# A third product of sums of vertical attention done as an addition on VectorE, with new due steps

## The chip, the cores and the metric

The kernel runs on one core of a Trainium2 chip. The core has five engines with a queue each: TensorE (PE, matrix products; PEld are its weight loads), VectorE (DVE), ScalarE (ACT), GpSimd (POOL) and SyncE (SP), which here only issues DMA transfers. An engine runs its instructions in the order in which they were written; semaphores hold an instruction back until what it needs is there. The metric is the device time of one execution in microseconds (us), lower is better.

## What is computed

Eight images of 64 x 64 pixels with 256 channels go through two layers; all is in fp32. The first layer, cut to what matters:

```python
q, k = split(x @ w_qkv + b_qkv)          # 2 x 256 channels; v = k
ctx_h = sdpa(h_windows(q), h_windows(k), h_windows(v))   # channels 0..127, windows of 8 rows
ctx_v = sdpa(v_windows(q), v_windows(k), v_windows(v))   # channels 128..255, windows of 8 columns
bias  = depthwise_conv3x3(hard_swish(v)) + dw_bias
x1    = hard_swish(concat(ctx_h, ctx_v) + bias) @ w_out + b_out
# sdpa(q,k,v): softmax(q k^T / sqrt(32)) v, four heads of 32, windows of 512 pixels
```

The second layer is global attention over the 4096 pixels of an image with 32 channels: f, g and h are products of x1 with weights divided by their spectral norm; the output is gamma * (softmax(g f^T) h @ wv + bv) + x1.

## The kernel before

Pixels are cut into eight blocks of 512. A **unit** is a window of one attention: eight horizontal ones (h, one for a block of rows), eight vertical ones (v) and two global ones (l, 2048 queries each) per image. A unit goes through steps, four in an h or v unit and 32 in an l unit. In a step TensorE makes scores of 128 keys against 512 queries for four heads at once (tile `s`, line 679, or 860 in an l unit); ScalarE takes two exponentials of 128x1024 (line 477, `weights_of`) and leaves the weights `p`, four heads side by side, in a ring of three buffers (pool `ptp`). One step later TensorE multiplies the weights of the step before with the values into `num` (line 696, or 876). Everything else is filled in between: a "fill".

The softmax's denominators are the sums of the weights over all keys. TensorE makes them as products with a matrix of ones (`sums`, line 714), 32 output rows for each head, in two halves of 256 columns. For an h or v unit it doesn't sum all four chunks so: VectorE first adds chunks 0 and 1 (`add`, line 705, 128x2048) into `acc`, which has one buffer, and three terms are left: chunk 2, chunk 3 and `acc`. For an l unit VectorE adds all 32 chunks (lines 885 and 887), and one term is left (line 896). ScalarE copies the sums out of PSUM (`copy_sums`, line 497); VectorE transposes, takes reciprocals, spreads them and multiplies (`norm`, lines 487 to 490 and 731).

Around it: projections of x to q and k (`project`, line 262, evicted by ScalarE on lines 551 to 570); the values' transpose on VectorE (line 632), written to DRAM and fetched by SP (lines 637 and 648); clip and swish into the padded image `hv` (lines 597 and 604), rings of two buffers for the lower channels and three for the upper, with borders set by POOL (lines 589 to 595, 609 and 610); the convolution, one tap on ScalarE (line 618) and eight taps on VectorE (line 622) for each pair of blocks and each half of the channels; a v unit's shuffle through DRAM (lines 737 and 742); join, clip and context (lines 755, 759 and 764); the projections to f, g and h (lines 783 and 810), of which h is transposed (line 824) and copied (line 825); and the output (lines 915, 262 and 925). Projections, sums and transposes share one PSUM bank, so that a fill waits for the eviction of the fill before.

The instructions' order is found at build time by a planner, `Flow`. Each piece of work is a task with a due step, tasks that it `needs` (their modelled end counts) and tasks that it comes `after` (only order counts). In each step the planner issues the scores, then the held values, and fills the engines' queues with waiting tasks by due step and by costs written at the head of the file. The dictionary `DUE` holds the due steps; most are relative to a unit's first step. Images overlap: projections and clips of the next image are made during the global attention of the one before, and so is its unit h[0], which stands ahead of the l units. A second copy of the whole attention (`exact`), with maxima taken out before the exponentials, stands behind a branch and isn't run with these inputs.

Whether an h or v unit adds chunk 2 on VectorE as well is already a switch, `adds_h` and `adds_v`: with it `acc` takes chunk 2 in a second addition (due at step `add2` of the unit) and two terms are left.

Of the kernel before, what the change touches and what calls it, by code (L numbers as in the profile page):

```python
# [23 lines left out]
NB = N // TB  # L24
# [7 lines left out]
def quad(r):  # L32
# [4 lines left out]
QH = 4  # L37

DUE = dict(
    near_k=-4, near_q=-3, near_values=-13, clip=-2, swish=4,  # L40
    conv_h0=13, conv_h1=10, conv_h2=7, conv_h3=16, conv_v0=-3, conv_v1=-3, conv_v2=14, conv_v3=9,
    tap=-5, join_h=14, join_hl=10, join_v=12, context=0, norm=2, release=0, sums=-2, add=1, adds_h=0, adds_v=0, add2=1, apart=4,
    fg0=-7, fg2=11, fg3=20, h0=3, h1=14, values_v=-3, near0=3, spread0=12, spread1=61,
    conv_first=-10, far_swish=1,
)
INSIDE = 4
AHEAD = 16
# [1 line left out]
HV = (2, 3)  # L49
# [216 lines left out]
def tile_attention_blocks(  # L266
# [108 lines left out]
    sums = prep.tile([P, NF + C + 1], F32, name="sums")  # L375
# [31 lines left out]
    def attention(images, load_x, out_rows, exact):  # L407
# [533 lines left out]
        flow = Flow()  # L941
# [103 lines left out]
        def behind(tag, bufs, first, *last):  # L1045
# [2 lines left out]
                first.after += queue[-bufs]  # L1048
            queue.append(last)

        loads = []

        def load(im, i, *tasks):
# [8 lines left out]
        def product_pieces(f, n, *end):  # L1062
            pieces = [(partial(f, k), [("pe", PROD / HALVES)]) for k in range(n * HALVES)]
            pieces[-1] = (pieces[-1][0], [("pe", PROD / HALVES), *end])
            return pieces

        def inside_due(i, far):

            n = i + min(i, INSIDE) + far
            return DUE["spread0"] + (DUE["spread1"] - DUE["spread0"]) * n // (NB + INSIDE)  # L1070

        for n, im in enumerate(ims):
            last = ims[n - 1] if n else None
            h, v, l = im.h, im.v, im.l
            near, far, sw, cv, pv = {}, {}, {}, {}, {}
            im.near, im.far = near, far
            for i in range(NB):
                u = h[i]
                after = [near[i - 1, 0], near[i - 1, 2]] if i else []
                after += [sw[i - QH, 0], pv[0, i - QH]] if i >= QH else []  # L1080

                inside = last and 0 < i <= INSIDE
                start = last.l[0].t if last else 0
                ready = start if inside else last.v[0].t + DUE["near0"] if last else max(0, u.t - 4)
                if i >= QH:
                    ready = max(ready, h[i - QH].t + 4)
                due = start + inside_due(i, 0) if inside else None
                for m in (0, 2):
                    near[i, m] = flow.add(
                        "pe", product_pieces(partial(im.project, i, m), 2, ("act", EVICT)),  # L1090
                        (u.t + DUE["near_k" if m else "near_q"]) if due is None else due, [], after, ready, True,
                    )
                early = start + inside_due(i, 0) if i in (1, 2) else u.t
                turned_v = flow.add(
                    "dve", [(partial(im.values, 0, i), [("dve", TAP), ("sp", ISSUE), ("dma", VIA)])],
                    min(early + 8, u.t + DUE["near_values"]), [near[i, 2]], [], min(early, u.t - 8),
                )
                pv[0, i] = flow.add(
                    "sp", [(partial(im.fetch_values, 0, i), [("sp", 4 * ISSUE), ("dma", FETCH)])], 0,
                    [turned_v], [], max(0, min(early, u.t - 3)),  # L1100
                )
                for m in (1, 3):
                    after = [sw[i - 1, 1]] if m == 3 and i else []
                    ready, due = (start, start + inside_due(i, 1)) if last else (0, u.t + 1)
                    end = (("act", 2 * (VIEW if m == 1 else EVICT)),)
                    far[i, m] = flow.add(
                        "pe", product_pieces(partial(im.project, i, m), 2, *end), due,
                        [], after, ready, True,
                    )
                for half in range(2):  # L1110
                    if half:
                        due = start + inside_due(i, 1) + DUE["far_swish"] if last else u.t + 6
                    else:
                        due = start + inside_due(i, 1) + DUE["swish"] - 2 if inside else u.t + DUE["swish"]
                    cl = flow.add(
                        "act", [(partial(im.clip, i, half), [("act", EVICT)])],
                        due + DUE["clip"] - 2, [far[i, 3] if half else near[i, 2]],
                        [cv[i // 2 - HV[half], half]] if i // 2 >= HV[half] else [],
                    )
                    sw[i, half] = flow.add(  # L1120
                        "dve", [(partial(im.swish, i, half), [("dve", SWISH), ("dma", HALO)])],
                        due, [cl], [sw[k, half] for k in (i - 1,) if i],
                    )
                    p = (i - 2) // 2 if i % 2 == 0 else i // 2 if i == NB - 1 else -1
                    if p >= 0:
                        k = 2 * p
                        due = (v if half else h)[k].t + DUE[f"conv_{'hv'[half]}{p}"]
                        if half and last and k == 0:
                            due = min(due, start + inside_due(2 * HV[1], 0) + DUE["conv_first"])
                        tap = flow.add(  # L1130
                            "act", [(partial(im.conv, p, half, (0,)), [("act", EXP)])],
                            due + DUE["tap"], [sw[q, half] for q in range(k, min(NB, k + 3))],
                            last.results[k] if last else [],
                        )
                        taps = [
                            (partial(im.conv, p, half, (q,)), [("dve", TAPS)]) for q in range(1, 9)
                        ]
                        cv[p, half] = flow.add("dve", taps, due, [tap])
            for i in range(NB):
                turned_v = flow.add(  # L1140
                    "dve", [(partial(im.values, 1, i), [("dve", TAP), ("sp", ISSUE), ("dma", VIA)])],
# [6 lines left out]
            context = {}  # L1148
            for kind, us in enumerate((h, v)):
                for i, u in enumerate(us):  # L1150
                    due = u.t + (DUE["join_v"] if kind else DUE["join_h"] if i < NQ else DUE["join_hl"] + 4 * (i - NQ))
# [9 lines left out]
            for kind, k in (("f", 0), ("f", 1), ("h", 0), ("f", 2), ("f", 3), ("h", 1)):  # L1161
                after = order[-1:]
                if kind == "f":
                    due = l[0].t + DUE[f"fg{max(0, k - 1) and k}"]
                    pf[k] = flow.add(
                        "pe", product_pieces(partial(im.project_fg, k), 2, ("act", EVICT)),
                        due, combined + [context[z, i] for z in range(2) for i in (2 * k, 2 * k + 1)],
                        [*after, *([turned[0]] if k == 3 else []), *([pf[0]] if k == 2 else [])], 0, True,
                    )
                    order.append(pf[k])  # L1170
                    pf[k] = flow.add("sp", [(partial(im.fetch_fg, k), [("sp", 10 * ISSUE), ("dma", FETCH)])], 0, [pf[k]])
                else:
                    due = l[0].t + DUE[f"h{k}"]
                    ph[k] = flow.add(
                        "pe", product_pieces(partial(im.project_h, k), 2, ("act", EVICT)),
                        due, [context[z, i] for z in range(2) for i in range(4 * k, 4 * k + 4)],
                        [*after, *([pf[2]] if k == 1 else [])], 0, True,
                    )
                    order.append(ph[k])
                    turned[k] = flow.add(  # L1180
                        "turn", [(partial(im.turn_h, k), [("pe", TURN), ("act", EVICT)])], due + 1, [ph[k]],
                        bank=True,
                    )
# [72 lines left out]
    xv = xT.rearrange("b (k p) n -> b p k n", p=P)  # L1256
    ov = out.rearrange("(b m p) n -> b m p n", m=2, p=P)
    attention(
        range(B),
        lambda b, i: xv[b, :, :, i * TB : (i + 1) * TB],  # L1260
# [18 lines left out]
    with tc.If(fine < 2 * P):  # L1279
        with tc.For_i(0, B) as b:  # L1280
            attention(
                [b],
                lambda b, i: xT[bass.ds(b, 1)].rearrange("o (k p) n -> p (o k) n", p=P)[
                    :, :, i * TB : (i + 1) * TB
                ],
                lambda b, m: out[bass.ds(b * C + m * P, P), :],
                exact=True,
            )
# [45 lines left out]
```

## Time and profile before

| What | us |
|---|---|
| median of three runs | 3434.96 (3431.73 to 3436.49) |
| the profiled execution's own time | 3432.03 |
| its span on the core | 3430.1 |
| PE busy | 3368.3 |
| DVE busy | 2729.4 |
| ACT busy | 2666.5 |
| POOL busy | 63.1 |

The span begins with the first and ends with the last recorded instruction of the core; the run's own time is 1.9 us more. An engine's busy time is the union of its instructions' times. The end of a matmul is modelled, so that a wait inside a run of matmuls can be counted as busy. The granted TensorE clock was 0.997 of full speed. An fp32 matmul of the program shows in the trace as two records. In the groups, a line gives the engine, the operation, the tile written and those read, shapes, the number of records, their busy time, the mean ns of one, and the engine's idle time just before them with what ended it.

### The profile page before, as it was taken

The numbers are of one execution on the slowest core, as the hardware profiler recorded it, in microseconds if no ns is written. First come the engines' busy times: TensorE is split into PE (matmuls) and PEld (weight loads), VectorE is DVE, ScalarE is ACT, GpSimd is POOL, SyncE is SP. The second block draws the span as 40 slices with busy tenths as digits, with TensorE's granted clock in tenths as the row PEclk, the third lists the DMA queues.
The fourth block names the chain that finished last, engine by engine and source line by source line (L and its number), as shares of the span: only waits on it lengthen the run. The fifth ranks groups of instructions, "written<-read, shape, count | busy, mean of one in ns | idle before, by whom it ended". The sixth has DMA issues, their size and how long they took to land.

```text
span 3430.1 us, 80125 instructions
## 1 busy us (share of the span) xinstructions
PE 3368.3 (98%) x34804; PEld 1154.6 (34%) x34804; DVE 2729.4 (80%) x2276; ACT 2666.5 (78%) x3235; POOL 63.1 (2%) x266
## 2 busy tenths in 40 slices
PE   8999999999999999999999999999999999999997
PEld 3333333333333333333333333333333333333322
DVE  4897798777897778968789687896878968788776
ACT  5788777887787877878778787787877878778875
POOL 0000000000000000000000000000000000000000
PEclk9999999999999999999999999999999999999998
DMA  2131103311123111231112311123111231122200
GB/s 71 57 99 51 56 28 88 96 46 50 44 72 100 48 45 44 72 106 41 50 50 75 98 37 47 56 81 92 40 38 59 84 86 40 38 72 65 70 31 26
DMA packets 249417, 209.94 MB, mean 61 GB/s; under 512 B 26080, under 2 KB 190432, under 8 KB 249056
## 3 DMA queue, kind: packets, MB, share of 16 engines
q1 hardware_dynamic: 246816, 204.18, 20.4%
q8 instruction: 275, 4.51, 0.6%
q10 hardware_dynamic: 2240, 0.56, 0.1%
q14 instruction: 86, 0.70, 0.1%
HBM read 99.78 MB, written 83.89 MB: 54 GB/s over the span
## 4 chain that ended last, share of the span: by engine, by line
PE 79%; DVE 14%; ACT 4%; issue 2%; DMA 1%; DVEq 0%; ACTq 0%; SPq 0%
PE s L679 16%; DVE acc_l L887 12%; PE pq L262 11%; PE s L860 10%; PE num_l L876 8%; PE num_v L696 7%; PE num_h L696 7%; PE s L262 6%; PE sum_h L714 5%; PE sum_v L714 5%; PE pf L783 2%; DVE act L622 1%; ACT p_l L477 1%; ACT p_h L477 1%; PE s L915 1%
## 5 line engine op out<-in xcount | busy, mean ns | idle before, releaser
L887 DVE TENSOR_TENSOR acc_l<-acc_l,p_l 128x2048 f32<-128x2048 f32 x480 | 1099.8, 2291 | 230.7 <-ACT p_l L477 207.6
L477 ACT ACTIVATE p_l<-s 128x1024 f32<-128x1024 f32 x1024 | 992.9, 1026 | 200.6 <-PE s L860 143.7
L622 DVE SCALAR_TENSOR_TENSOR act<-hv,dw_sb,act 128x1024 f32<-128x1024 f32 x512 | 655.7, 1281 | 22.7 <-ACT act L618 8.6
L860 PE MATMUL s<-gq,f 32*128 32x512 f32 x4096 | 625.9, 640 | 1.4 <-ACT ot_l L925 0.9
L477 ACT ACTIVATE p_h<-s 128x1024 f32<-128x1024 f32 x512 | 494.5, 1023 | 94.9 <-PE s L679 70.9
L477 ACT ACTIVATE p_v<-s 128x1024 f32<-128x1024 f32 x512 | 496.0, 1023 | 92.7 <-PE s L679 86.9
L876 PE MATMUL num_l<-p_l,h_sb 128*32 128x512 f32 x4096 | 546.4, 605 | 2.4 <-ACT nums_l L891 2.1
L262 PE MATMUL pq<-x,wqkv_sb 128*32 128x256 f32 x8192 | 524.0, 382 | 2.1 <-ACT qh L551 0.8
L262 PEld LDWEIGHTS pq<-x,wqkv_sb 128*32 128x32 f32 x8192 | 261.3, 110 | 368.9 <-issue 201.9
L679 PE MATMUL s<-qh,kh 32*128 32x512 f32 x2048 | 319.0, 641 | 10.3 <-ACT qh L551 5.9
L679 PE MATMUL s<-qv,kv 32*128 32x512 f32 x2048 | 317.7, 640 | 0.2 <-ACT p_v L477 0.2
L860 PEld LDWEIGHTS s<-gq,f 32*128 32x128 f32 x4096 | 192.9, 182 | 298.6 <-issue 284.7
L696 PE MATMUL num_v<-p_v,vs 128*32 128x512 f32 x2048 | 272.7, 605 | 2.5 <-DMA vs<-kvia 2.5
L696 PE MATMUL num_h<-p_h,vs 128*32 128x512 f32 x2048 | 271.6, 602 | 3.5 <-ACT nums_l L891 1.9
L262 PE MATMUL s<-act,wout_sb 128*32 128x512 f32 x2048 | 227.0, 595 | 0.0
L925 ACT ACTIVATE ot_l<-s,bias_o 128x512 f32<-128x512 f32 x128 | 81.2, 684 | 174.2 <-PE s L262 162.7
L876 PEld LDWEIGHTS num_l<-p_l,h_sb 128*32 128x32 f32 x4096 | 80.7, 108 | 387.5 <-issue 370.7
L705 DVE TENSOR_TENSOR acc_h<-p_h,p_h 128x2048 f32<-128x2048 f32 x64 | 146.5, 2290 | 44.1 <-ACT p_h L477 30.9
L705 DVE TENSOR_TENSOR acc_v<-p_v,p_v 128x2048 f32<-128x2048 f32 x64 | 146.6, 2291 | 36.8 <-ACT p_v L477 36.8
L679 PEld LDWEIGHTS s<-qh,kh 32*128 32x128 f32 x2048 | 97.1, 183 | 182.2 <-issue 146.7
L679 PEld LDWEIGHTS s<-qv,kv 32*128 32x128 f32 x2048 | 101.6, 182 | 162.2 <-issue 157.9
L714 PE MATMUL sum_h<-p_h,ones 128*32 128x256 f32 x2048 | 137.3, 380 | 4.2 <-ACT kv L570 4.2
(125 smaller groups left out, 2417.8 us busy)
## 6 DMA issues: line engine op xcount, KB each, us to landing
x<-in_xT SPq DMA_DIRECT2D x92, 512.0 KB, 3.9
kvia<-kt SPq DMA_DIRECT2D x128, 256.0 KB, 2.4
vs<-kvia SPq DMA_DIRECT2D x512, 64.0 KB, 2.1
out<-ot_l SPq DMA_DIRECT2D x128, 256.0 KB, 2.1
via_v<-nums_v SPq DMA_DIRECT2D x64, 256.0 KB, 2.1
shuf_v<-via_v SPq DMA_DIRECT2D x256, 64.0 KB, 2.0
f<-fg SPq DMA_DIRECT2D x256, 64.0 KB, 2.0
gq<-fg SPq DMA_DIRECT2D x64, 64.0 KB, 2.0
```

The costliest lines, as they stand in the source:

```text
L262: nc.tensor.matmul(out[quad(r), :], lhsT=lhsT[:, quad(r)], rhs=rhs, start=start, stop=stop)
L477: nc.scalar.activation(pt[:, 2 * z : 2 * z + 2, :], sc[z], AF.Exp, scale=scale)
L622: nc.vector.scalar_tensor_tensor(o, src, wt, o, ALU.mult, ALU.add)
L679: nc.tensor.matmul(row_of(sc, r), lhsT=k[quad(r), c * P : (c + 1) * P], rhs=q[quad(r), :], start=True, stop=not exact,)
L696: nc.tensor.matmul(u["num"][quad(r), :], lhsT=vs[kind, i][:, r, c, :], rhs=u[c][:, r, :], start=(c == 0), stop=(c == 3),)
L705: nc.vector.tensor_add(u["acc"], u["acc"] if c == 2 else u[0], u[c])
L714: nc.tensor.matmul(u["sum"][quad(r), cols], lhsT=ones[:, :D], rhs=pt[:, r, cols], start=(k == 0), stop=(k == len(of) - 1),)
L783: nc.tensor.matmul(pf[quad(r), cols], lhsT=wcomb[:, k, quad(r % 2)], rhs=act_of(2 * p + r // 2, k, cols), start=(k == 0), stop=(k == 1),)
L860: nc.tensor.matmul(row_of(sc, r), lhsT=f4[quad(r), c * P : (c + 1) * P], rhs=gq[quad(r), z, :], start=True, stop=not exact,)
L876: nc.tensor.matmul(u["num"][quad(r), :], lhsT=h_sb[:, c, :], rhs=u[c][:, r, :], start=(c == 0), stop=(c == 4 * NB - 1),)
L887: nc.vector.tensor_add(u["acc"], u["acc"], u[c])
L925: nc.scalar.activation(ot, po, AF.Identity, bias=bias_o[:, m : m + 1])
```

## The change

With `adds_v=1`, vertical units add chunk 2 into `acc` on VectorE, and TensorE's products with ones take two terms, chunk 3 and `acc`, in place of three. Horizontal units stay as they are. Twenty-odd due steps have other values, among them those of the convolutions of each pair of blocks, the clips and swishes, the sums, the near projections and f, g, h. Three orders are changed: a clip into an `hv` buffer now comes after the convolution that used that buffer before, over the border between images too (`convs` counts pairs over all images); `project_fg` of pair 2 comes after the fetch of pair 1 in place of pair 0; and `project_h` of each half comes after a fetch of f and g (of pair 0 for the first, of pair 2 for the second, which had it before).

```diff
 DUE = dict(
-    near_k=-4, near_q=-3, near_values=-13, clip=-2, swish=4,
-    conv_h0=13, conv_h1=10, conv_h2=7, conv_h3=16, conv_v0=-3, conv_v1=-3, conv_v2=14, conv_v3=9,
-    tap=-5, join_h=14, join_hl=10, join_v=12, context=0, norm=2, release=0, sums=-2, add=1, adds_h=0, adds_v=0, add2=1, apart=4,
-    fg0=-7, fg2=11, fg3=20, h0=3, h1=14, values_v=-3, near0=3, spread0=12, spread1=61,
-    conv_first=-10, far_swish=1,
+    near_k=-4, near_q=-1, near_values=-13, clip=-12, swish=-1,
+    conv_h0=17, conv_h1=15, conv_h2=7, conv_h3=14, conv_v0=1, conv_v1=10, conv_v2=14, conv_v3=12,
+    tap=-9, join_h=13, join_hl=10, join_v=12, context=0, norm=2, release=0, sums=0, add=1, adds_h=0, adds_v=1, add2=3, apart=4,
+    fg0=-7, fg2=5, fg3=20, h0=1, h1=10, values_v=-4, near0=-4, spread0=12, spread1=61,
+    conv_first=3, far_swish=1,
 )
...
+        convs = {}
         loads = []
...
                         due + DUE["clip"] - 2, [far[i, 3] if half else near[i, 2]],
-                        [cv[i // 2 - HV[half], half]] if i // 2 >= HV[half] else [],
+                        [k for k in (convs.get((i // 2 - HV[half] + n * NB // 2, half)),) if k],
...
-                        cv[p, half] = flow.add("dve", taps, due, [tap])
+                        cv[p, half] = convs[p + n * NB // 2, half] = flow.add("dve", taps, due, [tap])
...
-                        [*after, *([turned[0]] if k == 3 else []), *([pf[0]] if k == 2 else [])], 0, True,
+                        [*after, *([turned[0]] if k == 3 else []), *([pf[1]] if k == 2 else [])], 0, True,
...
-                        [*after, *([pf[2]] if k == 1 else [])], 0, True,
+                        [*after, pf[2 * k]], 0, True,
```

## The prediction

> **What bounds the kernel now.** I read the page's totals first, then busy time by stage, then the groups that the change touches, then the order of time inside one unit of vertical attention.
>
> ```profile
> span 3430.1 us, 80125 instructions
> ...
> PE 3368.3 (98%) x34804; PEld 1154.6 (34%) x34804; DVE 2729.4 (80%) x2276; ACT 2666.5 (78%) x3235; POOL 63.1 (2%) x266
> ```
>
> TensorE is busy all through; VectorE and ScalarE have a fifth free on average. By stage of the second image (horizontal, vertical and global attention; columns are length, then busy time of PE, PEld, DVE, ACT):
>
> ```profile
> 480.80:593.30 112.50, 111.24 (x1212) 39.80 (x1208) 98.22 (x102) 85.72 (x109) 4.06 (x20) 1.00 0.26 78
> 593.30:693.70 100.40, 99.33 (x1065) 35.72 (x1061) 77.41 (x84) 80.20 (x97) 0.18 (x2) 1.00 0.33 90
> 693.70:901.90 208.20, 207.93 (x2082) 67.96 (x2078) 164.18 (x97) 166.63 (x201) 3.35 (x10) 1.00 0.14 41
> ```
>
> VectorE is fullest in the horizontal stage (87%) and has 23.0 us idle in the vertical one. The groups of the change:
>
> ```profile
> L714 PE MATMUL sum_v<-p_v,ones 128*32 128x256 f32 x2048 | 135.2, 379 | 6.4 <-ACT h_sb L825 6.4
> L714 PE MATMUL sum_v<-acc_v,ones 128*32 128x256 f32 x1024 | 78.7, 379 | 0.0
> L705 DVE TENSOR_TENSOR acc_v<-p_v,p_v 128x2048 f32<-128x2048 f32 x64 | 146.6, 2291 | 36.8 <-ACT p_v L477 36.8
> L622 DVE SCALAR_TENSOR_TENSOR act<-hv,dw_sb,act 128x1024 f32<-128x1024 f32 x512 | 655.7, 1281 | 22.7 <-ACT act L618 8.6
> ```
>
> A row's 379 ns is no price, since matmuls overlap. The price is start to start, on TensorE's timeline of one vertical unit:
>
> ```profile
> 1057.57 1.14 PE L679 MATMUL s<-qv,kv 32*128 32x512 f32 x8
> ...
> 1059.64 1.37 PE L679 MATMUL s<-qv,kv 32*128 32x512 f32 x8
> ...
> 1061.94 1.51 PE L679 MATMUL s<-qv,kv 32*128 32x512 f32 x8
> ...
> 1064.38 1.14 PE L679 MATMUL s<-qv,kv 32*128 32x512 f32 x8
> ...
> 1066.33 1.05 PE L714 MATMUL sum_v<-p_v,ones 128*32 128x256 f32 x16
> 1067.19 0.61 PE L714 MATMUL sum_v<-acc_v,ones 128*32 128x256 f32 x8
> 1067.62 1.05 PE L714 MATMUL sum_v<-p_v,ones 128*32 128x256 f32 x16
> 1068.49 0.61 PE L714 MATMUL sum_v<-acc_v,ones 128*32 128x256 f32 x8
> 1069.03 1.14 PE L679 MATMUL s<-qv,kv 32*128 32x512 f32 x8
> ```
>
> A unit takes 11.46 us. Steps of scores and values alone last 2.07, then 2.30 and 2.44: the last two contain a wait of 0.2 to 0.4 us for ScalarE's exponentials, which "busy" hides. Eight recorded ones-matmuls cost 0.43 us. Last, two lines from the waits and from the end of the chain:
>
> ```profile
> PE sum_v L714 <- ACT h_sb L825: 6.4, 6, 1.1
> ```
>
> ```profile
> 3394.10 2.30 DVE acc_l L887
> ```
>
> The final global stage is a chain of VectorE additions, one every 2.4 us; work put in front of it shows in full.
>
> [...]
>
> **The change, part by part.**
>
> Products removed. The built order has 64 units with 16 products for sum_v instead of 24, so 16 records fewer per unit: 2 x 0.43 = 0.86 us. 64 x 0.86 = **-55.2 us**. Weights loads overlap and go with them.
>
> Additions added. 64 x 2.29 = 146.6 us of VectorE, 18.3 per image. The moved due steps make room: in the built order of a steady image the vertical stage keeps 9 of its 18 taps (-9 x 1.28 = -11.5), one normalization (-2.4) and one context product (-0.7) go past its end. VectorE there: 77.4 + 18.3 - 11.5 - 2.4 - 0.7 = 81.1. The stage's PE length: seven of its eight sums stand inside it, 7 x 0.86 = 6.0, and two projections (16 x 0.216 = 3.5) go to the horizontal stage: 100.4 - 6.0 - 3.5 = 90.9. So 89% full. The horizontal stage gets 8 taps: 98.2 + 10.2 = 108.5 in 112.5 + 3.5 = 116.0, 93% full. Hidden by TensorE's work; what little room is left is the question. The eight taps have a place: VectorE now idles 9.7 us in the second horizontal unit of that stage, and the changed order puts seven taps (9.0 us) there. Lags in this stage may cost 0 to 3 us an image (no gain: no work leaves it); I take 0.4 x 7 = **+3**.
>
> Inside a vertical unit. Sum products now stand one step later (after the next unit's second scores), so the steps are 2.07, 2.30, 2.44 and a last of 4.65 - 0.86 = 3.79: 10.60 us. ScalarE needs 8 x 0.92 + 2 x 0.59 + 0.72 = 9.3 of it. VectorE: two additions 4.6, normalization 2.5, join and context 1.4, transpose 0.7 = 9.2. The accumulator has one buffer, so the next first addition starts only when the sums are read, 0.1 us after the fill; then normalization, a join, the second addition: 0.1 + 2.3 + 2.5 + 0.7 + 2.3 = 7.9 us. The weights ring of three makes ScalarE's exponential of the next unit's second chunk wait for that addition; it wants to start at about 8.0. Behind it stand all later exponentials, and TensorE waits for those. Margin 0.1 us. Bounds: 0 to 0.5 us a unit; I take 0.1: **+6**. The sums themselves start at 8.8, after it.
>
> The wait for h_sb. Now the transposed h's eviction holds the one fill bank and the sum behind it waits 1.1 us. In the changed order a whole step lies between: **-6.4**, or 0 if another eviction takes its place.
>
> First image. Its vertical stage holds on VectorE 16 additions, 19 taps, 8 normalizations and 21 small operations (16 x 2.29 + 19 x 1.28 + 8 x 2.4 + 21 x 0.69 = 95 us) in 101.1 - 6.0 - 1.7 = 93.4 of TensorE (one projection of 1.7 leaves): over full. **+3**, between 0 and 6.
>
> Last image. The chain of additions gets two small operations more in front of it (1.4 us) and four taps in the unit before: **+2**, between 0 and 5.
>
> Guards and other due steps. ScalarE's clips and their memsets on POOL stand as many units behind the last tap of the buffer that they replace as now; near projections as far ahead of their scores; 0. On SP a normalization's store and its shuffled fetch go out some 6 us later; the fetch, behind the next transpose's store, lands some 1.5 us into the following unit, and the join reads it at 8: 6 us of cover. Without it the join would hold VectorE for what is missing. The store of values goes at most a place later and its fetch has two units.
>
> Sum: -55.2 + 3 + 6 - 6.4 + 3 + 2 = -47.6. The profiled execution took 3432.0 us (span 3430.1), so 3384.4; the median of the runs is 2.9 above it: **3387 us**.
>
> **Rivals.**
>
> A, the gain half lost: the second addition is late by 0.5 us in every vertical unit through the ring of weights, 64 x 0.5 = 32 instead of 6, giving 3413. For it: the margin of 0.1 us, and ScalarE already waited 53.3 us for acc_l through the same ring. Against it: taps are nearly gone from these units.
>
> B, slower: VectorE becomes the bound because its idle time can't be filled. Horizontal and vertical stage leave it 7.5 + 9.8 = 17.3 us per image; now it idles 14.3 + 23.0 = 37.3 there. If 30 of that were dependency gaps that stay, each of seven images would pay 12.7 for a gain of 8.8: 3435 + 27 = 3462. It decides from 26.1 us of unfillable idle time. For it: waits for clips and copies (85.7 and 84.1 us over all). Against it: five horizontal units in a row now run with gaps of 0.3 to 1.3 us in 11 to 23, so such queues do fill up.
>
> C, more than the products: the lags don't appear and the h_sb wait goes: -61.6, 3373.
>
> That the products stay is excluded by the built order.
>
> **How the numbers follow.** Forecast 0.55 (3373 to 3400 by its bounds), C 0.14, A 0.18, B with smaller losses that cancel the gain 0.13. Holding 8 in 10 takes in C and A, with some room on both sides: 3366 to 3418. Faster by over 0.2%, which is about what a measurement of this kernel can tell (below 3428): 0.88; within 0.2%: 0.03; slower: 0.09.
>
> **What would show it.** The group sum_v from p_v with 1024 records; acc_v with 128; vertical stages near 91 us with VectorE near 81; units 10.6 apart. The step on the ring is wrong if ScalarE's p_v waits long for acc_v (A: over 25 us). B shows as horizontal stages over 120 us with VectorE at 95% and TensorE waiting for p_h or sums for acc. The first vertical stage should be longer than the others, and the chain should still end in acc_l. The prediction falls if those stages are not shorter than now by 6 us or more.

## The result and the profile after

The changed kernel took 3422.61 us (median of seven runs, 3418.80 to 3425.57) against 3434.96 (3431.73 to 3437.63, seven runs): a ratio of 0.9966, interval 0.9954 to 0.9977. It is faster by 0.34%, a quarter of the 48 us that the forecast had. The profiled execution took 3424.4 us and its span is 3422.6, 7.5 less than the span before; stages are compared within these two spans. Each kernel's stages are read from one execution, and the changed kernel's seven lie up to 6.8 us apart, so a difference of a few us between the totals of two traces may be chance.

The totals on the page of the changed kernel:

```profile
span 3422.6 us, 78296 instructions
...
PE 3334.3 (97%) x33780; PEld 1126.0 (33%) x33780; DVE 2860.2 (84%) x2340; ACT 2665.0 (78%) x3235; POOL 63.5 (2%) x266
```

TensorE has 34.0 us less to do, but the span is only 7.5 shorter: 26.5 us of new idle time on TensorE, and more that "busy" hides. The groups of the change, in the changed kernel:

```profile
L705 DVE TENSOR_TENSOR acc_v<-p_v,p_v 128x2048 f32<-128x2048 f32 x64 | 146.7, 2292 | 87.1 <-issue 60.5 <-PE sum_v L714 17.3 <-ACT p_v L477 9.3
...
L705 DVE TENSOR_TENSOR acc_v<-acc_v,p_v 128x2048 f32<-128x2048 f32 x64 | 146.2, 2284 | 4.8 <-ACT p_v L477 4.8
...
L714 PE MATMUL sum_v<-p_v,ones 128*32 128x256 f32 x1024 | 80.1, 385 | 0.8 <-ACT fg L792 0.8
L714 PE MATMUL sum_v<-acc_v,ones 128*32 128x256 f32 x1024 | 79.2, 381 | 3.1 <-DVE acc_v L705 3.1
```

The 1024 records are gone and the 64 additions are there. The first line holds the surprise: before the *first* addition of a unit VectorE now idles 87.1 us in all, and before it was 36.8, all of it for the weights. Now it waits for the sums of the unit before, which read the one accumulator. The list of releasers names them for 17.3 us only, and has no releaser for 60.5 ("issue"); but each of the 42 waits that make up the 87.1 ends 0.12 to 0.14 us after the last of those sums.

The first two stages of the second image (horizontal, vertical; length, then busy time of PE, PEld, DVE, ACT):

```profile
506.20:621.80 115.60, 114.52 (x1280) 41.49 (x1276) 107.22 (x109) 88.63 (x112) 6.56 (x20) 1.00 0.26 81
621.80:713.40 91.60, 89.81 (x884) 30.24 (x880) 80.45 (x82) 77.20 (x92) 0.18 (x2) 1.00 0.32 91
```

And the first image's vertical stage, one line of the kernel before and one of the changed kernel, in the same columns (the clock that TensorE was granted is third from the end):

```profile
171.90:273.00 101.10, 98.64 (x1065) 35.45 (x1061) 89.64 (x96) 82.95 (x100) 0.52 (x5) 1.00 0.36 101
```

```profile
177.50:294.00 116.50, 101.70 (x916) 32.55 (x912) 89.44 (x90) 79.72 (x95) 0.45 (x5) 0.93 0.31 87
```

The stage has 149 matmul records less and lasts 15.4 us longer, and VectorE is *less* full than before (77% against 89%). So VectorE's load alone doesn't bound it there. Set against the terms of the forecast, image by image (from its first scores to those of the next; spans):

| | before | after | measured | forecast |
|---|---|---|---|---|
| start of the first scores | 22.0 | 20.0 | -2.0 | 0 |
| image 1 | 458.7 | 486.2 | +27.5 | -3.9 |
| images 2 to 7, mean of each | 421.5 | 416.3 | -5.2 | -6.5 |
| image 8 | 420.2 | 418.5 | -1.7 | -4.5 |

(The forecast of an image is -6.9 for the products, +0.75 for the ring, -0.8 for the h_sb wait; +3 in image 1; +3/7 for lags in the others; +2 in image 8.) Some 31 us of the miss lie in the first image, 8 in the six middle ones, 3 in the last. The earlier start, which takes 2 off, isn't put down to the change: over all kernels below it lies between 19.8 and 22.5 us without a pattern.

The length of a steady unit of the changed kernel on TensorE's timeline, from a third scores to the next unit's third (start, length):

```profile
1077.28 1.14 PE L679 MATMUL s<-qv,kv 32*128 32x512 f32 x8
...
1079.35 1.37 PE L679 MATMUL s<-qv,kv 32*128 32x512 f32 x8
...
1081.65 1.51 PE L679 MATMUL s<-qv,kv 32*128 32x512 f32 x8
...
1084.08 1.14 PE L679 MATMUL s<-qv,kv 32*128 32x512 f32 x8
1085.35 1.07 PE L696 MATMUL num_v<-p_v,vs 128*32 128x512 f32 x8
1086.23 0.61 PE L714 MATMUL sum_v<-p_v,ones 128*32 128x256 f32 x8
...
1088.07 1.14 PE L679 MATMUL s<-qv,kv 32*128 32x512 f32 x8
```

Steps of 2.07, 2.30, 2.43 and 3.99 us: 10.79 where the forecast had 10.60, and the 0.20 stand in the last step. There the first values of a unit (1085.35) now precede the sums of the unit before, and they wait for ScalarE to copy that unit's numerator out of its single PSUM buffer. The changed kernel's list of waits has it (us in total, times, longest):

```profile
PE num_v L696 <- ACT nums_v L726: 5.8, 22, 0.3
```

Before, the sums stood between and covered that copy: there the only wait of `num_v` on TensorE is one of 2.5 us, for a DMA. The wait for `h_sb` is gone, as forecast. The chain of work that ended last still closes the run with the global unit's additions, on VectorE (start, length):

```profile
3386.96 2.30 DVE acc_l L887
```

### The profile page after: what moved, and what is told of

Its sections match the earlier page's. It is cut to its first block, busy times and chain, and to the rows that moved or that the text cites. A ratio compares the mean times of both kernels' runs of the same rounds, so it can differ in the third digit from the quotient of the medians.

```text
span 3422.6 us, 78296 instructions
## 1 busy us (share of the span) xinstructions
PE 3334.3 (97%) x33780; PEld 1126.0 (33%) x33780; DVE 2860.2 (84%) x2340; ACT 2665.0 (78%) x3235; POOL 63.5 (2%) x266
## 4 chain that ended last, share of the span: by engine, by line
PE 70%; DVE 15%; ACT 8%; issue 4%; DMA 2%; SPq 1%; DVEq 0%; ACTq 0%
PE s L679 12%; DVE acc_l L887 11%; PE pq L262 11%; PE s L860 10%; PE num_l L876 9%; PE num_h L696 7%; PE s L262 6%; PE sum_h L714 5%; PE num_v L696 4%; ACT p_v L477 4%; PE sum_v L714 3%; DVE act L622 2%; PE pf L783 2%; ACT p_h L477 1%; PE s L915 1%
## 5 line engine op out<-in xcount | busy, mean ns | idle before, releaser
L679 PE MATMUL s<-qv,kv 32*128 32x512 f32 x2048 | 327.3, 644 | 2.4 <-ACT p_v L477 2.4
L705 DVE TENSOR_TENSOR acc_v<-p_v,p_v 128x2048 f32<-128x2048 f32 x64 | 146.7, 2292 | 87.1 <-issue 60.5
L679 PEld LDWEIGHTS s<-qv,kv 32*128 32x128 f32 x2048 | 106.8, 184 | 181.3 <-issue 172.1
L705 DVE TENSOR_TENSOR acc_v<-acc_v,p_v 128x2048 f32<-128x2048 f32 x64 | 146.2, 2284 | 4.8 <-ACT p_v L477 4.8
```

What stands on the lines that cost most here:

```text
L679: nc.tensor.matmul(row_of(sc, r), lhsT=k[quad(r), c * P : (c + 1) * P], rhs=q[quad(r), :], start=True, stop=not exact,)
L705: nc.vector.tensor_add(u["acc"], u["acc"] if c == 2 else u[0], u[c])
```

## The experiments

All kernels compute the full reference; they differ in where work is placed and in whether vertical sums take two terms or three. Ratios are to the kernel before, with 95% intervals.

**The two halves alone.** `due_alone` is the changed kernel with the old three products:

```diff
-    ... adds_h=0, adds_v=1, add2=3, ...
+    ... adds_h=0, adds_v=0, add2=3, ...
```

> All new due steps and orders, but three products everywhere as before. Theory 1: the first image loses some 10 us by the due steps, the others keep 421 us: about 3445. If the due steps carry the gain by themselves (waits removed, as that for h_sb): under 3430. If TensorE's products are the gain and nothing else matters: 3435.

3433.99 us, 0.9997 (0.9988 to 1.0006): no change in the total. Inside it, image 1 is 470.6 (11.8 more than before), the middle ones 420.6 (0.9 less each). The first image lost what was expected; the 3445 didn't come since the later images gave most of it back.

`add_alone` is the other half: the changed kernel's orders and the addition, with the old `DUE` line for line.

```diff
-    (the new values of DUE)
+    (the old values of DUE, with adds_v=1)
```

> The old due steps with the addition in all vertical units (its own step is the old add2). VectorE would have 77.4 + 18.3 = 95.7 us in a vertical stage of about 94 us. Theory 1: the stage stays near 97 to 100 us and sums or weights wait for the additions: 3415 to 3435. If room on VectorE doesn't matter: vertical stages of 94 us, about 3385.

3465.67 us, 1.0087 (1.0070 to 1.0104): slower by 31 us. None of the expectations had that. Image 1 takes 488.9, the middle ones 418.9, and the last 437.8, whose vertical and final stages are 10.1 and 7.5 us longer than before. What follows: in the middle images the addition pays even with the old steps (2.6 us each), and twice that with the new ones; the last image needs the new ones. But image 1 loses its 30 us here as well, with the old steps, so that loss isn't theirs alone.

**Image 1 treated apart.** `due_of` gives image 1 its own due steps; images 2 to 8 stay as changed. In `first_old` image 1 is as before, with old steps and three products; in `first_noadd` it has the new steps and three products.

```diff
+DUE0 = dict(...)            # first_old: the old values; first_noadd: the new, adds_v=0
+def due_of(n):
+    return DUE if n else DUE0
...
+            DUE = due_of(u.n)
```

> The changed kernel, but the first image keeps the due steps and the three products of before; images 2 to 8 are as changed. Theory 1 (the first image pays the loss: it has no global attention before it to hide its projections, so VectorE and the queues have no room for the additions and the moved work): the first three stages take 286 us again in place of 305, its global stage about 195 in place of 201, and the time is near 3398. Theory 2 (the loss is spread over all images by the ring of weights): near 3422, as the changed kernel.

3402.35 us, 0.9906 (0.9889 to 0.9922).

> The changed kernel, but the first image makes the third product on TensorE as before; its due steps are the new ones. If the eight additions are what overfills VectorE in the first image: first vertical stage near 103 us and the time near 3403. If the new due steps do it (three transposes of values in a row, late values for the first vertical unit): the 9 us ahead of the first values stay, vertical stage near 112, time near 3415.

3408.93 us, 0.9925 (0.9908 to 0.9941). So image 1 alone costs the changed kernel 20.3 us. Its parts by the traces: before 458.7; with the new steps 470.3 (11.6 more); with the additions too 486.2 (15.9 more). Of the 11.6, some 4 don't come from image 1's own steps: `first_old` keeps the old ones there and takes 463.0. The middle images are 416.6 and 416.2, 5 less than before.

**Two suspects in image 1.** One is the loop through the single accumulator. In an overloaded stage the overdue taps have earlier due steps than the unit's second addition and stand ahead of it; the sums wait for that addition, and the next first addition for the sums. `first_addfirst` puts both additions of image 1's vertical units ahead of the overdue work.

```diff
-"dve", [(partial(u.add, 1), ...)], u.t + 2, ...
+"dve", [(partial(u.add, 1), ...)], u.t + 2 - (30 if u.kind == "v" and not u.n else 0), ...
-"dve", [(partial(u.add, 2), ...)], u.t + DUE["add2"], ...
+"dve", [(partial(u.add, 2), ...)], u.t + DUE["add2"] - (30 if u.kind == "v" and not u.n else 0), ...
```

> The changed kernel, with one thing moved: in the first image's vertical units both additions get due steps 30 earlier, so that the planner puts the second addition right behind the normalization and the taps behind it; the work is the same. If the loop (addition, overdue taps, second addition, sums that free the one accumulator, next addition) makes the first vertical stage long: it falls from 116.6 to about 104, and the time to about 3411. If VectorE simply has too much work there, whatever its order: it stays at 114 or more, or the time comes back in the global stage, and the total stays at 3420.

3425.01 us, 0.9972 (0.9962 to 0.9981): no gain in all. The stage did fall from 116.6 to 102.7, but the global stage behind it grew by 2.4, and image 2's vertical stage took 103.1 instead of 91.7. There the planner now divided the sums of a unit over two steps, and VectorE waited 7.5 us for them at one place. By the list of waits of the whole run (its lines are shifted; L718 is the addition, L727 the sums):

```profile
DVE acc_v L718 <- PE sum_v L727: 19.5, 10, 7.5
```

A total that didn't move would have buried a right idea; the stages showed that the loss had changed its image. In image 1 the sums still stand a step late here, though undivided: less work between the two additions was enough to take 13.9 us off the stage.

The other suspect is late values. The new steps let image 1 transpose the values of three vertical units in a row; the third transpose waits 2.7 us for a free buffer, and three stores stand on SP ahead of the first fetch. `first_turn` lets image 1's transposes go five steps ahead of their unit, not eight.

```diff
-                    v[i].t + DUE["values_v"], [far[k, 3] for k in range(NB)], [], v[i].t - 8,
+                    v[i].t + DUE["values_v"], [far[k, 3] for k in range(NB)], [], v[i].t - (8 if n else 5),
```

> The changed kernel, with the values' transposes of the first image ready three steps later, so that two and not three stand in a row ahead of the first vertical unit. If the third transpose (which waits 2.7 us for a free buffer) and its store ahead of the first fetch on SP cause the 9 us gap before the first values: that gap falls by 4 to 6 us and the time to about 3417. If the late fetch is only where a lag shows that comes back elsewhere: 3422.

3412.80 us, 0.9939 (0.9922 to 0.9956): 9.8 us better than the changed kernel. TensorE's first vertical values in the changed kernel, and then in this one (its line 709 is 696; in brackets the idle time before and its releaser):

```profile
190.08 1.93 PE L696 MATMUL num_v<-p_v,vs 128*32 128x512 f32 x8 [6.82 <-DMA vs<-kvia]
```

```profile
186.61 1.94 PE L709 MATMUL num_v<-p_v,vs 128*32 128x512 f32 x8 [4.75 <-DMA vs<-kvia]
```

The wait lost only 2.1 us, yet the vertical stage fell by 9.8 (to 106.8) and the horizontal one by 3.2. So most of the gain came another way: with the transposes out of its way the planner placed the first unit's sums and most of the second additions earlier, and VectorE's idle time before the first additions of that stage fell from 18.2 to 7.5 us, ScalarE's wait for `acc_v` from 9.8 to 3.2. The mean clock of the stage rose from 0.93 to 0.97 with it.

**The place of the sums.** The kernel before issues a unit's sums right behind its last values; the changed one a step later, in image 1 for all seven units with a vertical one behind them, in the middle images for the first five. It is the addition that moves them: in `due_alone`, with the new due steps, they stand where they stood, and in `add_alone`, with the old ones, nearly all stand late. `forced_rel` has image 1 as in `first_old`, and in images 2 to 8 forces a vertical unit's sums, and the numerator's copy ahead of them on ScalarE, right behind its last values. The planner first places what a forced task needs, so the second addition moves forward on VectorE as well. `forced_all` has the addition and the forced sums in image 1 too, where the due steps are the old ones (with `add2=3`).

```diff
+        for k in [k for e in ("act", "pe") for k in self.lanes[e] if k.force == self.t]:
+            self.require(k)
...
+                total.force = e if u.kind == "v" and u.n else -1     # forced_all: without "and u.n"
...
+            u.released.force = e if u.kind == "v" and u.n else -1
```

> The kernel with the old first image, and in images 2 to 8 the sums of a vertical unit are issued one step earlier, behind the unit's last values, as they stood before the change. If the sums' later place is what costs the later images 1.3 us in each vertical stage (the copy of the numerators is no longer hidden behind the sums): units of 10.6 us and not 10.8, vertical stages near 91.0 in place of 92.3, time near 3394 in place of 3402. If the second addition can't be there that early: TensorE waits for acc, stages of 93 us or more, time above 3402.

3387.47 us, 0.9862 (0.9845 to 0.9878): 14.9 less than `first_old`. The middle images are 413.1 in place of 416.6, the vertical stage 90.0.

> As the one before, but the first image makes the addition too, with the due steps of before and the earlier sums. If the order of taps and additions is the whole trouble of the first image: first vertical stage near 98 us, time near 3388. If VectorE's load is: 110 us or more there, time above 3400.

3389.98 us, 0.9874 (0.9857 to 0.9890). Image 1, with additions, takes 465.4 and its vertical stage 104.1; with nearly the same due steps and the sums left to the planner that stage took 123.6 in `add_alone`.

Closest to a clean cut is `forced_new`: the changed kernel, all its due steps kept, with these forced sums and what they take along, the copy and the second addition.

> The changed kernel, due steps untouched, with one rule more: the sums of a vertical unit, with the release of its numerator ahead, stand right behind the unit's last values in all images. Theory 1 (the first image loses through the loop over the single accumulator, since its sums stand late): the first vertical stage falls from 116.6 us to about 105, the first horizontal one stays near 157.5, the later vertical stages are 90.0 instead of 92.2 and the total is 3394 (3389 to 3400). Theory 2 (the first stage is long because VectorE has too much to do there): it stays above 113, only the later images gain, total 3402 to 3406. Theory 3 (it is the late first values alone): as theory 2 in the total, with the loss in the first two units.

3387.18 us (3386.43 to 3388.74), 0.9863 (0.9846 to 0.9879): 35.4 us below the changed kernel. Its vertical stages of image 1 and image 2 by the trace:

```profile
177.40:276.80 99.40, 92.48 (x916) 30.78 (x912) 88.96 (x89) 79.40 (x95) 0.45 (x5) 0.97 0.37 103
```

```profile
604.80:694.80 90.00, 90.00 (x892) 30.15 (x888) 82.86 (x85) 78.07 (x94) 0.18 (x2) 1.00 0.35 99
```

The first has the same 916 records and the same VectorE work as in the changed kernel (88.96 against 89.44 us), in 99.4 instead of 116.5 us. The theory that VectorE had too much to do falls here. By images, against the changed kernel: 17.6 less in image 1, 3.3 less in each of six, 0.5 less in the last: 38, the whole difference of the spans. That the total is the forecast's own 3387 is chance: image 1 is still 13.8 us above its forecast, and the six middle ones are 2.0 each below theirs.

How the loop runs can be read in one unit of the changed kernel's first image, one of two there whose sums the planner divided over two steps. VectorE (in brackets the idle time before):

```profile
256.49 2.29 DVE L705 TENSOR_TENSOR acc_v<-p_v,p_v 128x2048 f32<-128x2048 f32 x1 [5.12 <-ACT p_v L477]
...
259.33 2.56 DVE L622 SCALAR_TENSOR_TENSOR act<-hv,dw_sb,act 128x1024 f32<-128x1024 f32 x2
...
265.99 2.28 DVE L705 TENSOR_TENSOR acc_v<-acc_v,p_v 128x2048 f32<-128x2048 f32 x1
...
273.61 2.29 DVE L705 TENSOR_TENSOR acc_v<-p_v,p_v 128x2048 f32<-128x2048 f32 x1 [4.74 <-PE sum_v L714]
```

TensorE in the same time:

```profile
268.33 0.70 PE L714 MATMUL sum_v<-acc_v,ones 128*32 128x256 f32 x8 [3.08 <-DVE acc_v L705]
...
269.81 2.09 PE L679 MATMUL s<-qv,kv 32*128 32x512 f32 x8
...
272.87 0.60 PE L714 MATMUL sum_v<-acc_v,ones 128*32 128x256 f32 x8
```

From one first addition to the next: 2.2 us for the addition itself, 7.3 of transposes, taps, contexts and the late normalization of the unit before, 2.2 for the second addition, and then 5.4 until the sums have let go of the accumulator, since their second half comes only behind the next scores and values. That is 17.1 us for a unit of nominally 10.6. TensorE waits 3.08 us for VectorE's second addition, then VectorE 4.74 for TensorE's sums: each stands still for the other, in turn, and neither is full. In the stage's eight units one to ten other instructions of VectorE stand between the two additions, in `forced_new` none to three. VectorE in the same stage there (its L708 is 705):

```profile
236.98 2.29 DVE L708 TENSOR_TENSOR acc_v<-p_v,p_v 128x2048 f32<-128x2048 f32 x1
...
240.98 2.28 DVE L708 TENSOR_TENSOR acc_v<-acc_v,p_v 128x2048 f32<-128x2048 f32 x1
...
247.96 2.29 DVE L708 TENSOR_TENSOR acc_v<-p_v,p_v 128x2048 f32<-128x2048 f32 x1
```

Both additions are over at 243.2, the sums follow at once, and VectorE's small work and the normalization fill the 4.7 us until the next first addition, which finds the accumulator free. It does so all through that run, where the 87.1 us of idle time are none:

```profile
L708 DVE TENSOR_TENSOR acc_v<-p_v,p_v 128x2048 f32<-128x2048 f32 x64 | 146.5, 2289 | 0.0
```

`forced_turn` joins this with the later transposes of `first_turn`.

> As forced_new, and in the first image the transposes of the vertical values may be taken 5 steps ahead of their unit at the earliest instead of 8. If the late first values and the loop are two losses apart, the gains add: some 10 us below forced_new, first horizontal stage 154.3, first vertical stage about 98 to 102, total 3384 (3380 to 3389). If they are one loss seen twice, the total is within 3 us of forced_new.

3385.57 us (3384.13 to 3388.64), 0.9859 (0.9843 to 0.9876): within 2 us of `forced_new`, and the ranges overlap, as for one loss seen twice. What the later transposes had gained was mostly the loop's loss. The late values themselves stay: TensorE still waits 4.6 us for the first ones, after 6.7 in `forced_new`.

Last, `whole_sums` keeps the planner from dividing a vertical unit's sums, and doesn't force their place.

```diff
+                whole = u.kind == "v" and terms == 2
+                if whole:
+                    pieces = [(partial(lambda u: [u.sums(n) for n in range(2 * HALVES)], u), [("pe", 2 * PROD), ("act", COPY)])]
```

> The changed kernel, but a vertical unit's 16 products of ones are placed as one piece, never divided over two steps; in the changed kernel two units of the first image have them divided. If the divided sums make the long units of the first stage (15 to 17 us) by holding the accumulator a step longer: first vertical stage 105 to 110 instead of 116.6, total 3411 to 3417. If it is the late place of all sums, divided or not, the stage stays at 114 to 117 and the total at 3420 to 3424. Later images have the same order as the changed kernel: 416.5 us each under both.

3414.95 us, 0.9943 (0.9927 to 0.9960): 7.7 below the changed kernel, the first vertical stage 107.6, the middle images 416.2, within 0.1 us of the changed kernel's. The stage is 9 us shorter, of the 17 which it loses against `forced_new`. That isn't the price of dividing alone: with whole sums the planner also put those of the sixth and seventh unit right behind their last values, and their second additions earlier. How the 17 us divide among divided sums, late sums and late second additions is not shown.

`forced_new` and `forced_turn` beat both kernels by 1.0% and 1.4%. A second accumulator would be another way to cut the loop; it wasn't tried.

## Why the forecast was wrong, step by step

**The step that failed** is "Inside a vertical unit", and with it the term "First image". The step saw that "sum products now stand one step later" and that the accumulator has one buffer. It then priced this for a steady unit alone, through the ring of weights, at 0.1 us: +6 us in all. The way back, from the late sums to the next unit's first addition, got no price. Placing the sums and the second addition earlier gives 38 us back in the spans, where the forecast missed by 40. The two figures don't cover the same loss, though: image 1 misses 13.8 more for other reasons, and with that loss taken out the middle images are 12 better than forecast.

- In the first image it is 17.6 us. The term "First image: +3, between 0 and 6" came from busy times, 95 us of VectorE in 93.4 of TensorE. VectorE was busy for 89.4, so the sum was 6 too high and the stage wasn't over full; yet it took 116.5. Old work stood between a unit's two additions, the sums came late and in part divided, and the length of this loop, not VectorE's load, set the pace. Three edits that shorten it in different ways, with nearly the same work, bring the stage to 102.7 (`first_addfirst`), 107.6 (`whole_sums`) and 99.4 (`forced_new`).
- In the middle images it is 3.3 us each (20 in all), 2.0 of it in the vertical stage. The copy of the numerator, which the sums used to hide, is the visible part: 0.2 us in five units, about 1 us an image. The rest wasn't traced to single waits. The ring, on which the step put its price, is not what binds: ScalarE's weights waited 9.8 us for `acc_v` in the whole run, all of it in the first image. Rival A had put its mark at 25. With forced sums the middle images are 8.5 us shorter than before, better than the 6.5 forecast. Of these 2.0, 1.2 are the forecast's charges for the ring and for lags, which then don't show; the rest stays open.

**The rest of the first image** is a second omission: the forecast set "guards and other due steps" to 0 on an argument about steady images. There it holds: `due_alone` gains 0.9 us in each. Image 1 of `due_alone` and `first_noadd` is 11.8 and 11.6 us longer than before with no addition at all (7.4 us of it in the horizontal stage), of which `first_old` shows 4.3 with image 1's old steps. Which of the nineteen moved steps do it isn't settled; TensorE's wait for the first vertical values, 6.8 us in `due_alone` and 2.5 before, is one visible part.

**Right by size:** the products: 1024 records fewer (64 x 0.86 is 55.0, not 55.2, which changes nothing). VectorE in the vertical stage, 80.5 against 81.1 forecast. The horizontal stage, 116.1 in most images against 116.0, so the lags (+3) didn't appear. The `h_sb` wait, 6.4 to none. The end of the chain. The last image misses by 3 us, but not by the work put before its final chain, which had +2: its final stage is only 0.9 longer. Rival B didn't come: no horizontal stage reached 120 us after the first image, and VectorE's gaps were filled. And the test "the prediction falls if those stages are not shorter than now by 6 us or more" was passed in steady images, 8.3 us, while the total failed: it looked at the wrong image.

## What to carry to other kernels

When a change adds a link to a loop over a single buffer, follow the loop once around through every engine's queue, and do it for the fullest stage, not the typical one: what stands in the queue between two links counts as part of the loop, like the 7.3 of 17.1 us in the unit read above. Read each stage's busy share after such a change; a stage that grew while no engine is full, as here at 77% of VectorE, is worth a look for engines that wait for each other in turn. And when the total doesn't move under an experiment, compare it stage by stage, since a gain in one place and a loss in another look alike from outside.

## What was unexpected in the hardware

TensorE's clock fell to half near waits of very different length. In the changed kernel's first vertical stage it is 0.50 in four stretches, one of 6.83 and three of 3.41 us. Two of them, each with the 3.41 us ahead of it, and last one in `first_old` (the first figure after the length is TensorE's busy time, the granted clock is third from the end):

```profile
231.23:234.64 3.41, 2.28 (x12) 0.54 (x14) 3.41 (x3) 2.45 (x3) 0.00 (x0) 1.00 0.19 60
234.64:238.05 3.41, 3.41 (x20) 0.62 (x16) 2.03 (x3) 1.91 (x3) 0.00 (x0) 0.50 0.30 87
265.36:268.77 3.41, 0.44 (x8) 0.29 (x12) 3.39 (x3) 0.38 (x1) 0.00 (x0) 1.00 0.36 81
268.77:272.18 3.41, 3.41 (x24) 0.93 (x20) 0.10 (x1) 1.74 (x3) 0.00 (x0) 0.50 0.80 225
```

```profile
180.29:183.70 3.41, 3.41 (x24) 0.99 (x16) 3.37 (x3) 0.00 (x0) 0.00 (x0) 0.50 0.02 6
```

The scores right behind the wait that ends at 268.33 take 2.09 us (269.81), those at 273.41, with the clock back at 1.00, take 1.14. TensorE's wait ahead of 268.77 is 3.08 us; ahead of 234.64 it counts as busy for 2.28 of 3.41 us, with one wait of 1.13; and in the 10.2 us ahead of another of the four, at 282.43, no wait is longer than 0.47 us. The length of a wait alone doesn't decide: in the kernel before, the clock stayed at 1.00 after one of 2.46 us. What decides isn't shown here. An upper estimate of the cost, from the mean clock of 0.93: 0.07 x 116.5 = 8 us of that stage, half of what it lost. With the sums forced it is 0.03 x 99.4 = 3 us, so up to 5 of the 17 us that forcing gains there come through the clock. The forecast had no such term.
